# An encoder's attention: where the batch norm's fold-in is issued, and how the denominators of the first two blocks are summed

## Chip, cores, metric

One core of one Trainium2 chip. The metric is device time in microseconds from launch to end, as the median of several runs. Besides, one execution was profiled; its page and trace are what is read here. The engines are TensorE (PE, with its weight loads PEld), VectorE (DVE), ScalarE (ACT), GpSimd (POOL) and SyncE (SP); SP, ACT and POOL issue DMAs.

## What is computed

Two graph layers over 4096 nodes with 512 features in 4 heads of 128. The change lies in the first half of layer 0, the "encoder". Cut to what matters, with `adj` a 0/1 matrix of 4096 x 4096:

```python
Xw  = einsum('hnd,hde->hne', Xh, W)
f1, f2 = Xw . V[:, 0], Xw . V[:, 1]
sig = sigmoid(f1[:, :, None] + f2[:, None, :])
att = masked_softmax(adj * sig, adj != 0)        # local and long-range patterns are the same here
Xa  = einsum('hij,hjd->hid', att, Xw)            # per head
Xn  = batchnorm(Xa as (n, 512), gamma, beta)     # mean and variance over the nodes
emb = batchnorm(elu(Xn @ enc_W.T + enc_b) + Xn)
```

The decoder (`att` once more, on `emb`) and a GAT layer with its own attention follow; the change doesn't touch their instructions.

## The kernel before

The attention runs over 8 **blocks**: head h = 0 to 3, and for each head two halves of 2048 target nodes (`blocks`, n = 0 to 7; below block 1 to 8). Each block has 32 **tiles** j of 128 source nodes. A tile `e` is 128 sources x 2048 targets in fp32. It is made by tanh on ACT (line 419), exp on ACT (420) and a multiplication by the mask tile `a` on DVE (421). PE multiplies it with the values in four products of 512 targets (351; the fourth bank is only taken at tile EVICT = 2, which makes up for tiles 0 and 1 at 348).

Buffers for `e`: eight in turn, so that tile j + 8 is written where tile j was. Mask tiles: five buffers, loaded from DRAM by SP (199) out of a byte copy of the adjacency, which POOL's casting DMAs (450) write while the kernel starts. Every fifth tile (j = 4, 9, ...) is kept for the decoder by an `ekeep` DMA that ACT's queue issues at tile j + 3 (338).

The softmax's **denominators** are sums over the sources. There are three ways to add a tile, and the pair that `modes(n)` returns chooses: a tile in the first tuple ("moved") is added by an accumulating DMA of POOL into `acc2` (363); one in the second ("by ones") by four small ones-matmuls of PE into the bank `den` (303); any other by DVE into `acc` (371). At a block's end `acc` and `acc2`, if there is one, go through ones-matmuls too.

The **ending** of a block is spread over the next block's tiles by `at(j, ...)`: at tile 2 DVE evicts the four banks (520), at INVERT = 4 it copies `den`, and POOL writes it to DRAM and reads it back as a column (248, 250); at tile 10 `invert_them` inverts that on DVE (254, 255) and writes it (256); at tiles 11, 12, 18 and 19 `spread` loads it as rows `rb` (261), and six tiles after each DVE scales the output (524) and takes its statistics for the batch norm (527).

The batch norm is folded into the next product: `bn_coefs` (163) makes a and b from the statistics, with a square root on ACT (160) among DVE operations; b times the weights is added to the bias by 12 small matmuls (539, 541), and each row block of the weights `w` is multiplied by a (534). In block 8 the coefficients of heads 0 to 2 are ready to be made, and `three_heads` does all of that at one place, tile 16; the last head's follow in `last_head`.

All engines work through their instructions in a fixed order that the framework settles before the run, from the program's order, the data dependencies and the `pinned` hints.

Of the kernel before, what the change touches and what calls it, by code (L numbers as in the profile page):

```python
# [34 lines left out]
ALU = mybir.AluOpType  # L35
# [4 lines left out]
N, F, H, D, P = 4096, 512, 4, 128, 128  # L40
IB = 512
NIB = N // IB
NJ = N // P
C = IB // P

TB = 2048
NTB = N // TB
# [9 lines left out]
TINY = 1e-30  # L57
# [1 line left out]
G_MAX = 75.0  # L59


ENC_FIRST = (), (5, 6, 10, 11, 15, 16, 20, 21, 25, 26, 30, 31)
ENC = (0, 2, 5, 7, 10, 12, 15, 17, 20, 22, 25), (8, 9, 30, 31)
GAT = (0, 2, 5, 7, 10, 12, 15, 17, 20, 22, 25), (9, 30, 31)

# [4 lines left out]
EVICT = 2  # L70
INVERT = 4
# [9 lines left out]
def kernel(ctx, tc, x, xT, adjT, w0, w0T, v0, wencT, wdecT, vecs, w1, w1T, a1, outT):  # L81
    nc = tc.nc
# [11 lines left out]
    def nodes(r, ib):  # L94
        return r[:, ib * IB:(ib + 1) * IB]

    def block(r, j):
        return r[:, j * D:(j + 1) * D]

    def bank():  # L100
        return psum.tile([P, IB], FP, name="ps")

    def bank1():
        return psum1.tile([P, IB], FP, name="den")
# [10 lines left out]
    def vec_of(name):  # L115
        return vec[:, VECS.index(name), :]
# [21 lines left out]
    bias = consts.tile([P, C], FP, name="bias")  # L138
# [24 lines left out]
    def bn_coefs(st, gamma, beta, a, b, lo, hi):  # L163

        mv = consts.tile([P, C, 2], FP, name="bmv", bufs=2)
        for fb in range(lo, hi):
            nc.vector.bn_aggr(mv[:, fb, :], st[:, fb].rearrange("p c s -> p (c s)"))
        a, b, mv = a[:, lo:hi], b[:, lo:hi], mv[:, lo:hi]
        rsqrt(a, mv[:, :, 1], BN_EPS)
        nc.vector.tensor_mul(a, a, vec_of(gamma)[:, lo:hi])  # L170
        nc.vector.tensor_mul(b, mv[:, :, 0], a)
        return nc.vector.tensor_sub(b, vec_of(beta)[:, lo:hi], b)
# [37 lines left out]
    def attention(what, keep, pools, weights, values, row_of, out, finish, ebufs, modes=None, invert=None,  # L210
                  kept=None, sums=None, sums2=None, extras={}, row0=None, masks0=()):
# [20 lines left out]
        spool, made, masks0 = pools, 0, list(masks0)  # L232
# [11 lines left out]
        def denominators(h, tb, den):  # L244

            dsb = spool.tile([P, IB], FP, name="dsb")
            (nc.vector.tensor_copy if kept is not None else nc.scalar.copy)(dsb, den)
            nc.gpsimd.dma_start(dens[h][tb], dsb[0:P:32, :])
            dcol = spool.tile([P, TB // P], FP, name="dcol", bufs=2)
            nc.gpsimd.dma_start(dcol, dens[h][tb].rearrange("s (q k) -> (s q) k", k=TB // P))  # L250
            return dcol
# [6 lines left out]
        def spread(h, tb, s):  # L258

            rb = spool.tile([P, IB], FP, name="rb", bufs=2)  # L260
            nc.gpsimd.dma_start(rb, everywhere(rinvs[h][tb], 0, s * IB, IB))  # L261
            return rb

        def at(j, f, *args):

            later.setdefault(j, []).append(lambda: f(*args))

        def ending(h, tb, po, den):

            outs = [out(spool, h, tb, s, po[s]) for s in range(SB)]  # L270
            if den is not None:
                def invert_later():
                    dcol = denominators(h, tb, den)
                    at(INVERT + 6, invert_them, h, tb, dcol)

                at(INVERT, invert_later)
            rbs = {}
            for s, o in enumerate(outs):

                j = INVERT + 7 + s % 2 + s // 2 * 7  # L280
                at(j, lambda s=s: rbs.update({s: spread(h, tb, s)}))
                for k, f in enumerate(finish):
                    at(j + 6 + k, lambda f=f, s=s, o=o: f(spool, h, tb, s, o, rbs[s], False))
# [9 lines left out]
        for n, (h, tb) in enumerate(blocks):  # L293
            last = n == len(blocks) - 1
            moved, by_ones = modes(n) if modes is not None else ((), ())
            if invert is not None:
                den = bank1()
# [9 lines left out]
            po, ahead = [bank() for _ in range(SB - 1)], []  # L307
# [80 lines left out]
                else:  # L388
                    at(EVICT, nc.scalar.dma_start, ekeep[h][tb][k], t)
            if not last:  # L390
                at(EVICT, lambda *block_end: ending(*block_end), h, tb, po, den if invert is not None else None)
                rowb = next_row
                continue
            outs = [out(spool, h, tb, s, po[s]) for s in range(SB)]
# [31 lines left out]
    with tc.tile_pool(name="keep", bufs=1) as keep:  # L426

        with tc.tile_pool(name="f_small", bufs=1) as small, tc.tile_pool(name="f_work", bufs=2) as work:
# [5 lines left out]
            for ib in range(NIB):  # L434
# [7 lines left out]
                for c in range(0, C, 1 if ib == 0 else C):  # L442
                    n = 1 if ib == 0 else C
                    load = nc.sync.dma_start(xs[ib][:, c:c + n, :], xin[:, c:c + n, :])
# [10 lines left out]
            for ib in range(NIB):  # L455
# [39 lines left out]
                for c in range(C):  # L495
                    j = ib * C + c
# [7 lines left out]
                if ib == SB - 1:  # L504
                    store_rows(rows[0], targets(0))
                    row0 = keep.tile([P, TB], FP, name="rowb", bufs=2)
                    row0_load = load_row(row0, rows[0], 0)
                    with tc.issue_after(row0_load.ins):
                        masks0 = []
# [23 lines left out]
        def scale_weights(fb):  # L533
            nc.vector.tensor_scalar_mul(w[:, fb, :], w[:, fb, :], a_att[:, fb:fb + 1])  # L534

        def add_to_bias(pb, lo, hi, base):
            for o in range(C):
                for fb in range(lo, hi):
                    nc.tensor.matmul(pb[:, o:o + 1], w[:, fb, o * P:(o + 1) * P], b_att[:, fb:fb + 1],
                                     start=(fb == lo), stop=(fb == hi - 1))  # L540
            nc.vector.tensor_add(bias, pb[:, 0:C], base)

        def three_heads(load):
            bn_coefs(stats, "enc_bn_gamma", "enc_bn_beta", a_att, b_att, 0, C - 1)
            add_to_bias(bank(), 0, C - 1, vec_of("enc_mlp_b"))
            for fb in range(C - 1):
                scale_weights(fb)

        with tc.tile_pool(name="enc", bufs=1) as spool:

            with tc.issue_after(last_act.ins), tc.issue_after(masks0[-1][1].ins):
                attention("enc", keep, spool, tanh_weights, R[0:4], lambda h, tb: (rows[tb], h), out_enc,
                          (scaled, statistics), 6, lambda n: ENC if n > 1 else ENC_FIRST, (TINY, ALU.max), "write",
                          row0=row0, masks0=masks0,
                          extras={(2, 8): encoder_weights, (H * NTB - 1, NJ // 2): three_heads})


        def mlp_block(work, w, src, dst, gamma, beta, scale, between, early=None):
# [40 lines left out]
        with tc.tile_pool(name="m_small", bufs=1) as small, tc.tile_pool(name="m_work", bufs=3) as work:  # L599
            yc = [R[3]] + [small.tile([P, N], FP, name=f"yc{o}") for o in range(1, C)]  # L600

            def last_head():
                bn_coefs(stats, "enc_bn_gamma", "enc_bn_beta", a_att, b_att, C - 1, C)
                add_to_bias(bank1(), C - 1, C, bias)
                scale_weights(C - 1)

            mlp_block(work, w, xc, yc, "enc_mlp_bn_gamma", "enc_mlp_bn_beta", a_att, lambda o, ib: None, last_head)


            for h in range(H):  # L610
                w2 = work.tile([P, D], FP, name="w2", bufs=2)
                nc.vector.tensor_scalar_mul(w2, w0Ts[:, h, :], a_mlp[:, h:h + 1])
                bb = work.tile([P, P], FP, name="bb", bufs=1)
                nc.vector.tensor_scalar_mul(bb, ones, b_mlp[:, h:h + 1])
                pc = bank1()
                nc.tensor.matmul(pc[:, 0:D], bb, w0Ts[:, h, :], start=True, stop=True)
                cr = work.tile([P, 1, D], FP, name="cr", bufs=2)
                nc.vector.tensor_copy(cr[:, 0, :], pc[:, 0:D])
                for ib in range(NIB):
                    pv = bank().rearrange("p (c d) -> p c d", d=D)  # L620
                    for c in range(C):
                        nc.tensor.matmul(pv[:, c, :], block(yc[h], ib * C + c), w2, start=True, stop=True)  # L622
                    nc.vector.tensor_add(nodes(xc[h], ib).rearrange("p (c d) -> p c d", d=D), pv,
                                         cr.to_broadcast([P, C, D]))
# [17 lines left out]
        with tc.tile_pool(name="dec", bufs=1) as spool:  # L642
            attention("dec", keep, spool, tanh_weights, xc, lambda h, tb: (rows[tb], h), out_dec, (scaled, elu), 4,
                      kept="read")
# [5 lines left out]
    with tc.tile_pool(name="l_small", bufs=1) as small, tc.tile_pool(name="l_work", bufs=2) as work:  # L650
        x1 = [R[2]] + [small.tile([P, N], FP, name=f"x1_{o}") for o in range(1, C)]

        pb = bank1()
# [86 lines left out]
        for ib in range(NIB):  # L740
            for c in range(C):
# [3 lines left out]
                j = ib * C + c  # L745
# [18 lines left out]
            if ib == SB - 1:  # L764
                store_rows(rows1[0], targets(0))
                row0 = w.rearrange("p c f -> p (c f)")
# [61 lines left out]
    with tc.tile_pool(name="gat", bufs=1) as spool:  # L828
        x1_last = []

        def load_last(load):
            x1_last.append(spool.tile([P, TB], FP, name="rowb", bufs=2))
            nc.sync.dma_start(x1_last[0], outT[(H - 1) * P:H * P, (NTB - 1) * TB:NTB * TB])

        attention("gat", spool, spool, gat_weights, v1, lambda h, tb: (rowsg, tb * H + h), out_gat,
                  (scaled_gat, add_to_output), 7, lambda n: GAT, (N * TINY, ALU.add), sums=R[2][:, 0:TB],
                  sums2=row0, row0=row0,
                  extras={(0, 1): rest_of_rows, (H * NTB - 1, NJ - 10): load_last})
# [42 lines left out]
```

## Time and profile before

| | |
|---|---|
| runs | 3296.29 us median of 6 (3295.82 to 3298.07) |
| profiled execution | 3295.82 us, span 3293.7 us |
| granted TensorE clock | 0.992 |
| busy: PE, DVE, ACT, POOL | 3214.0, 2681.7, 2599.3, 331.8 us |
| tanh and exp on ACT | 1968 and 1879 ns each |
| multiplication by the mask, add to `acc`, DVE | 2260 and 2287 ns each |
| encoder's attention | from about 67 to 1063 us of the span |

A line of groups reads: line, engine, operation, output<-inputs, shapes, count, busy time, mean ns of one, idle time before and what ended it. A line of waits reads: who waited, for whom, total us, times, longest. A line of the timeline reads: start, length, engine, line, operation, and in brackets the wait before it and what ended it. The chain of waits follows the work that ended last back to what released it. Matmuls are pipelined, so busy PE is not PE at its peak.

### The profile page before, as it was taken

What the parts mean: (1) busy time and instruction counts of PE and PEld (TensorE: products, weight loads), DVE (VectorE), ACT (ScalarE), POOL (GpSimd) and SP (SyncE); (2) the same over time, 40 slices, a digit from 0 to 9 for tenths busy, and PEclk for the clock granted to TensorE, in tenths of its full rate; (3) what the DMA queues carried; (4) which work ended last, traced back from release to release, by engine and by line L of the source; (5) the groups of instructions that cost most, each with busy time, mean ns of one, the idle gap of its engine ahead of it and who ended that gap; (6) DMA issues with size and microseconds to landing.
All of it is one profiled execution on the core that took longest, in us unless ns stands there. A gap on an engine that the chain in (4) does not pass through costs nothing.

```text
span 3293.7 us, 25880 instructions
## 1 busy us (share of the span) xinstructions
PE 3214.0 (98%) x8847; PEld 1487.9 (45%) x8847; DVE 2681.7 (81%) x1919; ACT 2599.3 (79%) x1901; POOL 331.8 (10%) x478
## 2 busy tenths in 40 slices
PE   7999999999999999999999999999999999999999
PEld 6333444444443464444444444448644444444443
DVE  6889999999998665656655665585699999999997
ACT  7999999999997449999999999565756556666663
POOL 2000110110110000000000000025201111111111
PEclk9999999999999999999999999999999999999999
DMA  9994988988986013434443444231379779788976
GB/s 206 196 191 144 256 223 233 259 223 233 265 233 163 4 62 125 152 126 137 141 151 127 135 142 138 63 134 72 93 195 226 175 196 218 193 194 206 220 188 147
DMA packets 180164, 558.54 MB, mean 170 GB/s; under 512 B 20356, under 2 KB 23684, under 8 KB 144192
## 3 DMA queue, kind: packets, MB, share of 16 engines
q0 software_dynamic: 43088, 210.09, 33.3%
q1 hardware_dynamic: 126432, 293.72, 26.3%
q10 hardware_dynamic: 10512, 53.08, 3.9%
q8 instruction: 69, 1.13, 0.1%
q14 instruction: 63, 0.52, 0.0%
HBM read 378.15 MB, written 95.82 MB: 144 GB/s over the span
## 4 chain that ended last, share of the span: by engine, by line
PE 62%; DVE 16%; issue 8%; ACT 7%; DMA 6%; SPq 0%; DVEq 0%; POOL 0%; ACTq 0%; POOLq 0%
PE ps L351 49%; PE ps L566 7%; DVE e L421 6%; ACT e L419 4%; DMA a<-mask 3%; DVE e L808 3%; PE ps L750 3%; DVE R L371 3%; ACT e L420 2%; DVE acc L371 2%; PE den L303 1%; PE ps L622 1%; DMA R<-in_x 1%; PE ps L348 1%; DMA rb<-rinvs 1%
## 5 line engine op out<-in xcount | busy, mean ns | idle before, releaser
L351 PE MATMUL ps<-e,R 128*128 128x512 f32 x6048 | 2631.7, 596 | 44.4 <-DVE e L421 31.7
L351 PEld LDWEIGHTS ps<-e,R 128*128 128x128 f32 x6048 | 1146.7, 191 | 1521.7 <-issue 1420.0
L421 DVE TENSOR_TENSOR e<-e,a 128x2048 f32<-128x2048 f32 (+1 forms) x470 | 1052.1, 2260 | 385.3 <-ACT e L420 363.3
L419 ACT ACTIVATE e<-rowb,score 128x2048 f32<-128x2048 f32 (+1 forms) x470 | 912.9, 1968 | 98.3 <-PE ps L351 58.1
L420 ACT ACTIVATE e<-e 128x2048 f32<-128x2048 f32 (+1 forms) x470 | 871.0, 1879 | 15.9 <-DVE e L421 9.7
L807 ACT ACTIVATE e<-rowb,nq,jcol 128x2048 f32<-128x2048 f32 x224 | 458.2, 2087 | 230.5 <-DMA w<-e 142.9
L808 DVE SCALAR_TENSOR_TENSOR e<-e,jcol,a 128x2048 f32<-128x2048 f32 (+1 forms) x259 | 592.5, 2326 | 2.6 <-ACT e L807 2.6
L371 DVE TENSOR_TENSOR R<-R,e 128x2048 f32<-128x2048 f32 x128 | 293.3, 2292 | 0.0
L371 DVE TENSOR_TENSOR acc<-acc,e 128x2048 f32<-128x2048 f32 x126 | 288.2, 2287 | 2.1
L566 PE MATMUL ps<-R,w 128*128 128x512 f32 x512 | 220.3, 592 | 0.6 <-DVE w L534 0.6
L261 POOL DMA_DIRECT2D rb<-rinvs x88 | 59.1, 687 | 1104.6 <-DVE R L524 894.6
L566 PEld LDWEIGHTS ps<-R,w 128*128 128x128 f32 x512 | 97.2, 190 | 122.7 <-issue 118.2
L363 POOL DMA_DIRECT2D w<-e x77 | 64.7, 841 | 645.8 <-DMA w<-e 268.5
L750 PE MATMUL ps<-w1x,hT 128*128 128x260 f32 x512 | 118.0, 390 | 1.8 <-ACT hT L723 1.8
L586 ACT ACTIVATE ex<-ps,bias 128x512 f32<-128x512 f32 x64 | 44.0, 688 | 95.4 <-PE ps L566 78.3
L363 POOL DMA_DIRECT2D acc<-e x66 | 55.8, 845 | 572.0 <-DMA acc<-e 167.0
L750 PEld LDWEIGHTS ps<-w1x,hT 128*128 128x128 f32 x512 | 98.3, 193 | 21.5 <-ACT hT L723 3.4
L807 ACT ACTIVATE e<-w,nq,jcol 128x2048 f32<-128x2048 f32 (+1 forms) x35 | 65.3, 1936 | 31.9 <-DMA dacc<-e 31.9
L820 ACT ACTIVATE R<-R,vec 128x512 f32<-128x512 f32 x32 | 23.0, 720 | 70.3 <-DVE R L817 70.2
L588 DVE SCALAR_TENSOR_TENSOR ex<-ex,re 128x512 f32<-128x512 f32 x64 | 45.0, 703 | 35.8 <-ACT re L587 35.6
L303 PE MATMUL den<-e,ones 128*32 128x512 f32 x584 | 70.9, 599 | 0.0
L755 ACT ACTIVATE R<-ps,rstd 128x128 f32<-128x128 f32 x128 | 38.5, 369 | 39.5 <-PE ps L750 37.3
(163 smaller groups left out, 1267.4 us busy)
## 6 DMA issues: line engine op xcount, KB each, us to landing
a<-mask SPq DMA_DIRECT2D x720, 256.0 KB, 3.6
w<-e POOLq DMA_DIRECT2D x77, 1024.0 KB, 8.3
acc<-e POOLq DMA_DIRECT2D x66, 1024.0 KB, 8.7
ekeep<-e ACTq DMA_DIRECT2D x48, 1024.0 KB, 5.5
e<-ekeep SPq DMA_DIRECT2D x48, 1024.0 KB, 4.8
rb<-rinvs POOLq DMA_DIRECT2D x88, 256.0 KB, 5.4
mask<-in_adjT POOLq DMA_DIRECT2D x8, 2048.0 KB, 103.7
rowb<-rows SPq DMA_DIRECT2D x16, 1024.0 KB, 4.9
```

The lines of the kernel that those rows point to most:

```text
L261: nc.gpsimd.dma_start(rb, everywhere(rinvs[h][tb], 0, s * IB, IB))
L303: last_ones = nc.tensor.matmul(den[s * 32:(s + 1) * 32, :], ones[:, 0:32], t[:, s * IB:(s + 1) * IB], start=not begun, stop=stop)
L351: last_main = nc.tensor.matmul(b, block(values[h], j), e[:, s * IB:(s + 1) * IB], start=(j == 0), stop=(j == NJ - 1))
L363: nc.gpsimd.dma_start(sums2 if n else dacc, e, **({"accum_op": ALU.add} if j > moved[0] else {}))
L371: nc.vector.tensor_add(acc, acc, e)
L419: nc.scalar.activation(e, rowb, AF.Tanh, bias=column(score[:, 1], j, h), scale=0.5)
L420: last_act = nc.scalar.activation(e, e, AF.Exp, scale=0.5)
L421: last_dve = nc.vector.tensor_mul(e, e, a)
L566: nc.tensor.matmul(z, w[:, fb, o * P:(o + 1) * P], nodes(src[fb], ib), start=(fb == 0), stop=(fb == C - 1))
L750: nc.tensor.matmul(b[:, 0:2 * DX], hT[:, fb, c * P:(c + 1) * P], w1x[:, fb, 2 * k:2 * k + 2, :].rearrange("p h x -> p (h x)"), start=(fb = ...
L807: last_act = nc.scalar.activation(e, rowb, AF.Relu, bias=column(nq, j, h), scale=column(jcol, j, h))
L808: last_dve = nc.vector.scalar_tensor_tensor(e, e, column(jcol2, j, h), a, ALU.add, ALU.mult)
```

## The change

It has four parts.

1. Block 1: the ones-tiles become 6, 7, 14, 15, 22, 23, 30 and 31 (eight in place of twelve). The other 24 tiles are added by DVE.
2. Block 1's ending, which runs in block 2: `slack` = 4, so `invert_them`, `spread` and what follows them come four tiles later. The endings of the other blocks stay.
3. Block 2: six tiles are moved by DMA (13, 15, 17, 20, 22, 25), six stay with PE (5, 6, 10, 11, 30, 31).
4. Block 8: `three_heads` becomes `coefs_of_three` at tile 10, `bias_of_three` at tile 12 and `scale_three` (bias addition and scaling of the weights) at tile 20. The bias matmuls' bank is held from 12 to 20.

```diff
-ENC_FIRST = (), (5, 6, 10, 11, 15, 16, 20, 21, 25, 26, 30, 31)
+ENC_FIRST = (), (6, 7, 14, 15, 22, 23, 30, 31)
+ENC_SECOND = (13, 15, 17, 20, 22, 25), (5, 6, 10, 11, 30, 31)
 ENC = (0, 2, 5, 7, 10, 12, 15, 17, 20, 22, 25), (8, 9, 30, 31)
...
-        def ending(h, tb, po, den):
+        def ending(h, tb, po, den, slack):
...
-                    at(INVERT + 6, invert_them, h, tb, dcol)
+                    at(INVERT + slack + 6, invert_them, h, tb, dcol)
...
-                j = INVERT + 7 + s % 2 + s // 2 * 7
+                j = INVERT + slack + 7 + s % 2 + s // 2 * 7
...
-                at(EVICT, lambda *block_end: ending(*block_end), h, tb, po, den if invert is not None else None)
+                at(EVICT, ending, h, tb, po, den if invert is not None else None,
+                   4 if kept == "write" and n == 0 else 0)
...
-        def add_to_bias(pb, lo, hi, base):
+        def bias_of(pb, lo, hi):
             for o in range(C):
                 for fb in range(lo, hi):
                     nc.tensor.matmul(pb[:, o:o + 1], w[:, fb, o * P:(o + 1) * P], b_att[:, fb:fb + 1],
                                      start=(fb == lo), stop=(fb == hi - 1))
-            nc.vector.tensor_add(bias, pb[:, 0:C], base)
-
-        def three_heads(load):
+            return pb
+        banks = []
+        def coefs_of_three(load):
             bn_coefs(stats, "enc_bn_gamma", "enc_bn_beta", a_att, b_att, 0, C - 1)
-            add_to_bias(bank(), 0, C - 1, vec_of("enc_mlp_b"))
+        def bias_of_three(load):
+            banks.append(bias_of(bank(), 0, C - 1))
+        def scale_three(load):
+            nc.vector.tensor_add(bias, banks[0][:, 0:C], vec_of("enc_mlp_b"))
             for fb in range(C - 1):
                 scale_weights(fb)
...
-                          (scaled, statistics), 6, lambda n: ENC if n > 1 else ENC_FIRST, (TINY, ALU.max), "write",
-                          row0=row0, masks0=masks0,
-                          extras={(2, 8): encoder_weights, (H * NTB - 1, NJ // 2): three_heads})
+                          (scaled, statistics), 6, lambda n: (ENC_FIRST, ENC_SECOND, ENC)[min(n, 2)],
+                          (TINY, ALU.max), "write", row0=row0, masks0=masks0,
+                          extras={(2, 8): encoder_weights, (H * NTB - 1, 10): coefs_of_three,
+                                  (H * NTB - 1, 12): bias_of_three, (H * NTB - 1, 20): scale_three})
```

The last head's `last_head` adds its bias in the same way as before, spelled with `bias_of`.

More of the change, by code (lines that the diff above doesn't have):

```diff
@@ L603, in last_head @@
                 bn_coefs(stats, "enc_bn_gamma", "enc_bn_beta", a_att, b_att, C - 1, C)
-                add_to_bias(bank1(), C - 1, C, bias)
+                nc.vector.tensor_add(bias, bias_of(bank1(), C - 1, C)[:, 0:C], bias)
                 scale_weights(C - 1)
```

## The prediction

> Blocks are numbered 1 to 8 as in the title (n = 0 to 7 in the code), tiles 0 to 31 in a block. The forecast is a small gain, 3286.6 us against 3296.29 us.
>
> **What bounds the kernel now.** I cut the encoder's attention at the start of each block's first tanh on ACT and asked for busy time by stretch. The columns are length, then busy time (count) of PE, weight loads, DVE, ACT and POOL, then TensorE clock, DMA share and GB/s. The rows are blocks 1, 2, 4, 7 and 8 (the last short of its final exp).
>
> ```profile
> 67.20:189.00 121.80, 111.12 (x311) 45.10 (x311) 104.28 (x58) 121.60 (x83) 0.00 (x0) 0.97 1.05 188
> 189.00:320.00 131.00, 126.63 (x360) 51.63 (x359) 123.61 (x68) 118.82 (x65) 3.89 (x7) 0.97 0.66 163
> 440.50:559.20 118.70, 116.18 (x305) 49.66 (x304) 114.57 (x65) 118.58 (x65) 13.24 (x18) 1.00 0.88 237
> 796.80:915.90 119.10, 116.55 (x306) 49.85 (x305) 114.94 (x65) 118.82 (x65) 13.20 (x18) 1.00 0.87 239
> 915.90:1040.80 124.90, 118.59 (x321) 51.24 (x320) 112.71 (x74) 119.59 (x67) 13.18 (x18) 0.97 0.84 225
> ```
>
> A steady block is ACT-bound: ACT is busy 118.58 of 118.70 us (tanh 1.97 plus exp 1.88 us per tile), with PE and DVE 2 to 4 us below. Blocks 2 and 8 stick out, by 12 and 6 us, while ACT has no more work there. What ACT waits for comes from the waits of two stretches: the first line is of 67 to 189 us, the others of 189 to 330 us; the numbers are total, times, longest.
>
> ```profile
> DVE e L421 <- DMA a<-mask: 8.3, 2, 6.6
> ...
> ACT e L420 <- DVE e L421: 6.3, 2, 3.8
> ACT e L419 <- DVE e L421: 4.9, 1, 4.9
> DVE dcol L254 <- DMA dcol<-dens: 4.4, 1, 4.4
> DVE e L421 <- DMA a<-mask: 2.7, 2, 1.7
> ```
>
> ACT loses 11.2 us to DVE in block 2. These are stores of kept tiles: ACT issues the `ekeep` DMA of tile j when it is three tiles on, in order with its activations, and that DMA waits for DVE's multiplication of j. Once DVE is over 11 us behind ACT, ACT stops. DVE itself lost 11.0 us to mask loads (8.3 + 2.7) and 4.4 us to the read-back of the first denominators. The chain of waits (start, length) shows both:
>
> ```profile
> 139.75 22.82 DMA a<-mask
> ...
> 165.01 17.41 DMA a<-mask
> ...
> 189.47 16.01 DMA a<-mask
> ...
> 239.78 6.44 DMA dcol<-dens
> ```
>
> While the adjacency is copied (DMA share 1.05 in block 1) a mask takes 16 to 23 us, and with five mask buffers the load for tile j+5 is issued when tile j is multiplied. That loop, not DVE's work, sets the pace from 140 to 206 us. In block 8 the timeline (start, length, engine, what; in brackets the wait) shows the batch norm of three heads:
>
> ```profile
> 983.98 0.20 ACT L160 ACTIVATE coefs<-coefs 128x3 f32<-128x3 f32 x1 [1.87 <-DVE coefs L159]
> ...
> 992.66 2.73 PE L539 MATMUL ps<-coefs,w 128*128 128x1 f32 x24
> ...
> 994.99 0.49 DVE L534 TENSOR_SCALAR w<-w,coefs 128x512 f32<-128x512 f32 x1 [7.58 <-PE ps L539]
> ...
> 1007.41 1.91 ACT L420 ACTIVATE e<-e 128x2048 f32<-128x2048 f32 x1 [3.34 <-DVE e L421]
> ```
>
> PE is some two tiles behind, the bias matmuls stand behind its backlog, and DVE, whose scaling of `w` must wait for them, stands 7.58 us; the ACT stall of 3.34 us is again a store behind a late multiplication. Ahead of that DVE has room, waiting twice for ACT (tiles 10 and 13):
>
> ```profile
> 958.54 4.50 DVE L421 TENSOR_TENSOR e<-e,a 128x2048 f32<-128x2048 f32 x2 [2.04 <-ACT e L420]
> ...
> 969.76 4.50 DVE L421 TENSOR_TENSOR e<-e,a 128x2048 f32<-128x2048 f32 x2 [2.20 <-ACT e L420]
> ```
>
> **The Trainium skill.** "VectorE: DVE Perf Modes", section "The TRN2 errata", prices an fp32 add of 2048 elements at 2291 ns; the accumulator adds here take 2287 ns. "ScalarE: Activation LUTs", section "What ACT_TABLE_LOAD costs", gives 1283 ns for the load plus about 1380 ns of drain per switch; here a load takes 1283 ns and starts 0.01 us after the tanh before it, so I price a switch at 1.28 us. "DMA: Bandwidth & Descriptors", section "Issuing engines are not separate DMA queues", says that transfers of SP, ACT and POOL interleave on the same engines; the mask loads above agree, since they land 2.5 us after issue at best, 11.3 in the median of 67 to 320 us. "TensorE: Matmul & The Clock Gate", Part 3, says that column tiles run concurrently; the 16 instructions of two ones-tiles take 1.92 us together, so a ones-tile costs PE about 0.95 us, not four full matmuls.
>
> **Part 1, fewer ones-tiles in block 1.** Tiles 5, 10, 11, 16, 20, 21, 25, 26 become DVE adds; 7, 14, 22, 23 become ones-tiles. PE loses 4 x 0.95 = 3.8 us, which I cost at nothing: DVE and the masks release PE there. DVE gains 4 x 2.29 = 9.2 us. Pushing the adds through the list of starts, DVE has four extra by tile 21 and is ready for tile 22 at 164.0 instead of 156.1 us (two short waits of 0.5 and 0.7 us swallow the rest); before, it waited there until 162.7. Tiles 22 and 23 then give two adds back, 25 and 26 take them again, within the 1.75 us mask wait at tile 27 and the 0.99 and 1.74 us at the next block's first two tiles. So the cover is the 11.0 us of mask waits. What can leak is the loop: tile 17's multiplication, which releases tile 22's load, ends 1.8 us later by the same count. If loads are limited by bandwidth, nothing moves; if by latency, all later landings move 1.8 us. I take 0.9. If the cover were gone altogether, block 2 would start 8 us later on DVE.
>
> **Part 2, first denominators later.** In block 2 `invert_them` moves from tile 10 to 14, the four `spread` loads and their eight DVE operations four tiles on. The read-back landed at 246.2 us, since the 8 KB write queued behind the last adjacency copies; DVE gets to tile 14 near 254 us. The 4.4 us wait goes, and nothing takes its place: invert, `rinvs`, `rb` (1 to 10 us each on POOL) have seven tiles, 27 us, until the first scaling at tile 21, and the last statistics come at tile 30.
>
> **Part 3, six moved tiles in block 2.** DVE keeps 19 adds. PE drops six ones-tiles and gains one for the DMA's sum: 5 x 0.95 = 4.8 us less, in a stretch (251 to 390 us) where the chain runs through a saturated PE. Of this I count 1.1 us: DVE's four waits for the evicted banks at 334 us. POOL gains six 1 MB accumulating DMAs, after the copies have ended at 239 us; each takes some 8.7 us to land and holds its buffer until then. A buffer is wanted again eight tiles (31 us) later. In block 4 the same six run beside six more with no ACT wait, so I cost them at nothing (they only add, so below nothing is excluded; the upper end is rival (c)). Queued behind a moved tile on POOL are `rinvs` and `rb`; their seven tiles cover it. The next block's first moved tile now waits for PE's last denominator, as in blocks 4 to 8 already (up to 25 us on POOL, ACT not held).
>
> Blocks 1 to 3: DVE, the bound until ACT leads again in block 3, gains 4.4 + 1.1 - 0.9 = **4.6 us**. ACT could gain 6.3 in block 2 and 1.5 in block 3 (waits for PE's denominator, 1.0, and an accumulating DMA, 0.5), so DVE's figure decides. The 4.9 us stall at block 2's tile 8 stays: it comes from tile 4, ahead of every edit but Part 1.
>
> **Part 4, block 8.** Coefficients at tile 10, bias matmuls at 12, scaling at 20. PE's 24 matmuls (2.73 us) find coefficients some 10 us old; DVE's scaling comes some 25 us after them; the bank is held eight tiles longer with four of seven others in use. From tile 13 DVE works without a pause, so its chain sets the end: block 8's last multiplication ends 138.1 us after the block's first tanh (915.9 to 1054.0), block 4's 127.7 us (440.5 to 568.2). The 10.4 us between are the wait of 7.58, the aggregate and small operations (0.82 and 0.79) and 1.6 of bias and scaling. The 1.6 stays; the aggregate falls into the 2.04 and 2.20 us of room. But the square root costs ACT two table loads and 0.20, 2.77 us, plus a wait of 0 to 1.87. At tile 17 DVE was late anyway; at tile 10 it follows ACT at once, so 2.8 to 4.6 us enter the chain, 3.7 taken. 10.4 - 1.6 - 3.7 = **5.1 us**, between 4.2 and 6.0.
>
> **The sum.** 4.6 + 5.1 = 9.7 us. The profiled execution took 3295.82 us (span 3293.7, 2.1 around it), 0.5 below the median; so it would be 3286.1, the median 3286.6.
>
> **The rivals.** (a) The mask loop doesn't absorb the adds: 8 us late on DVE by block 2. DVE then reaches the read-back after 246.2 us, so the 4.4 us wait would have gone anyway; blocks 1 to 3 lose 8 - 4.4 - 1.1 = 2.5, block 8 gains 5.1, in all 3293.7. For it: the chain alternates mask and multiplication. Against: a DMA share of 1.05 says that bytes, not requests, set landings. (b) The end is ACT's: all 7.8 us of blocks 2 and 3 and 6 of block 8 come back, 3282.5. For it: PE gets lighter. Against: nothing shortens DVE's list. (c) Slower: POOL's queue. If a `spread` that waits for DVE's first scaling (19.8 us now) is put ahead of the moved tiles 17 to 22, their buffers come back late: a tile is ready some 16 us after its tanh began, 8.7 to land leaves 6 us, and the rest of 19.8 is 13.8 us of ACT wait; a second one at tile 23 adds up to 5. Against 9.7 of gain that is 4 to 9 us more than now: about 3303. It decides once such a hold exceeds 6 us. Against: in block 4 moved tiles are issued ahead of the same loads. (d) A part has no effect, because the static order puts the new steps where the old stood: block 8 or block 2 alone gains, about 3291.5.
>
> **The numbers.** 0.2% is 6.6 us, about what a measurement of this kernel can tell from no change: faster means below 3289.7. Forecast 0.60, (a) 0.12, (b) 0.14, (c) 0.07, (d) 0.07. The forecast's own bounds (3.7 to 5.5 and 4.2 to 6.0) all lie beyond the line; for an order of instructions that I can't foresee I leave an eighth of it short of it. Faster 0.60 x 7/8 + 0.14 = 0.66, slower 0.07 from (c), same 0.27. The range 3281.0 to 3295.0 holds all but (c) and the edges.
>
> **What would show it.** Right: block 2 near 125 us with no `dcol` wait and ACT's later two stalls gone; mask waits in blocks 1 and 2 shrunk to 2 or 3 us with block 1's ACT time unchanged; block 8 near 121 us with no DVE wait at L534. Wrong: ACT waits in block 1, ACT waiting for an accumulating DMA in block 2, or block 8's ACT waiting for the square root by more than 2 us.

## The result, and the profile after

The changed kernel takes 3285.62 us in the median (20 runs, 3278.94 to 3292.59), the kernel before 3295.85 us beside it (40 runs). The ratio is 0.9971, with a 95% interval of 0.9965 to 0.9977: 9.6 us less, between 7.6 and 11.5. The forecast was 9.7 us less. Its parts did not come out as forecast, though, as the profile after already shows.

Its span is 3284.2 us. Not all of the 9.5 us to the span before is the change's: the first tanh starts at 63.6 instead of 67.2 us, ahead of every edit, and 3.2 us lie behind the last multiplication of block 8. Between the two this profile is only 2.7 us shorter (984.1 against 986.8): 6.2 less in block 8, but 1.4 more in blocks 1 to 3, and 2.1 more in blocks 4 to 7, which no edit touches. One profile of each kernel thus doesn't place the gain; what each part is worth is taken from the timed runs of the experiments, and the profiles say which waits came and went.

In the changed kernel the same steps stand on other lines: tanh, exp and the multiplication on 422, 423 and 424, the products on 352, the ones-matmuls on 304, the moved tiles on 364, DVE's adds on 372. These are the stretches of blocks 1, 2, 3, 4 and 8 (length; busy time and count of PE, weight loads, DVE, ACT, POOL; clock, DMA share, GB/s):

```profile
63.60:185.40 121.80, 108.73 (x283) 44.88 (x283) 112.06 (x62) 121.60 (x82) 0.00 (x0) 0.97 1.05 189
185.40:312.80 127.40, 121.99 (x322) 51.09 (x320) 125.37 (x68) 119.07 (x65) 8.97 (x13) 1.00 0.93 219
312.80:438.30 125.50, 119.29 (x306) 50.32 (x307) 116.15 (x65) 118.99 (x66) 13.20 (x18) 0.99 0.87 238
438.30:557.00 118.70, 114.80 (x301) 48.70 (x300) 112.70 (x63) 118.57 (x65) 13.18 (x18) 1.00 0.88 237
915.80:1035.70 119.90, 118.10 (x324) 51.87 (x322) 114.28 (x75) 119.72 (x68) 13.20 (x18) 0.99 0.86 235
```

Block 3 of the kernel before was this:

```profile
320.00:440.50 120.50, 119.89 (x308) 51.57 (x307) 115.14 (x65) 118.89 (x66) 13.23 (x18) 1.00 0.88 245
```

Block 8 went from 124.9 to 119.9 us and block 2 from 131.0 to 127.4, but block 3 from 120.5 to 125.5: the first three blocks together take 374.7 us against 373.3. The waits of block 1 (first line), of block 2 (next three) and of block 3 (last two) say where:

```profile
DVE e L424 <- DMA a<-mask: 1.6, 2, 1.2
...
ACT e L422 <- DVE e L424: 3.9, 1, 3.9
ACT e L422 <- DMA acc<-e: 2.6, 2, 2.3
...
DVE e L424 <- DMA a<-mask: 1.7, 1, 1.7
...
POOL acc L364 <- DMA acc<-e: 41.8, 5, 12.4
...
ACT e L422 <- DMA acc<-e: 6.4, 3, 3.3
```

The wait for the read-back (`dcol`) and ACT's two later stalls behind stores are gone, mask waits fell from 11.0 to 3.4 us (1.6 + 1.7, rounded), and block 1 still takes 121.80 us. ACT now waits for buffers which accumulating DMAs hold, 2.6 us in block 2 and 6.4 in block 3 (before, 0.5 in block 3 alone). The timeline of block 3 from 379 us on, ACT, POOL and SP alone (start, length, what, wait before):

```profile
379.17 2.00 ACT L422 ACTIVATE e<-rowb,score 128x2048 f32<-128x2048 f32 x1 [3.33 <-DMA acc<-e]
...
379.61 0.88 POOL L364 DMA_DIRECT2D acc<-e  x1 [10.25 <-DMA acc<-e]
...
380.56 1.22 SPq L193 DMA_DIRECT2D rowb<-rows  x1
...
392.40 2.00 ACT L422 ACTIVATE e<-rowb,score 128x2048 f32<-128x2048 f32 x1 [1.90 <-DMA acc<-e]
...
392.87 0.85 POOL L364 DMA_DIRECT2D acc<-e  x1 [12.38 <-DMA acc<-e]
```

Each accumulation waits for the one before. ACT's first wait, 3.33 us, ends as the accumulation issued at 368.42 lands, ahead of the row load. The next one, issued at 379.61, runs beside that 1 MB load (380.56) and takes 12.7 us, against 8.6 in the median; ACT's wait of 1.90 us at 392.40 ends as it lands. In block 8 the three steps stand apart:

```profile
957.92 0.20 ACT L161 ACTIVATE coefs<-coefs 128x3 f32<-128x3 f32 x1
...
961.38 4.50 DVE L424 TENSOR_TENSOR e<-e,a 128x2048 f32<-128x2048 f32 x2 [2.46 <-ACT e L423]
...
969.66 2.84 PE L542 MATMUL ps<-coefs,w 128*128 128x1 f32 x24
...
972.60 4.50 DVE L424 TENSOR_TENSOR e<-e,a 128x2048 f32<-128x2048 f32 x2 [2.20 <-ACT e L423]
...
1001.66 1.27 DVE L537 TENSOR_SCALAR w<-w,coefs 128x512 f32<-128x512 f32 x3
```

The square root waits for nothing, the scaling at 1001.66 carries no wait (7.58 before), and DVE still has its two gaps. From the block's first tanh to its last multiplication it takes 131.9 us (915.8 to 1047.7), against 138.1.

### The profile page after: what moved, and what is told of

Read it like the earlier page. It is cut to its first block, busy times and chain, and to the rows that moved or that the text cites. A ratio compares the mean times of both kernels' runs of the same rounds, so it can differ in the third digit from the quotient of the medians.

```text
span 3284.2 us, 25758 instructions
## 1 busy us (share of the span) xinstructions
PE 3203.1 (98%) x8775; PEld 1485.7 (45%) x8775; DVE 2691.9 (82%) x1923; ACT 2598.8 (79%) x1901; POOL 336.1 (10%) x484
## 4 chain that ended last, share of the span: by engine, by line
PE 67%; DVE 14%; ACT 7%; issue 7%; DMA 5%; SPq 0%; DVEq 0%; ACTq 0%; POOL 0%; POOLq 0%
PE ps L352 52%; DVE e L424 7%; PE ps L579 7%; ACT e L422 4%; PE ps L763 3%; DVE acc L372 3%; ACT e L423 2%; DMA a<-mask 2%; PE den L304 1%; DMA acc<-e 1%; DVE e L821 1%; DVE R L372 1%; PE ps L349 1%; PE ps L635 1%; DMA R<-in_x 1%
## 5 line engine op out<-in xcount | busy, mean ns | idle before, releaser
L372 DVE TENSOR_TENSOR acc<-acc,e 128x2048 f32<-128x2048 f32 x130 | 297.3, 2287 | 2.1
L304 PE MATMUL den<-e,ones 128*32 128x512 f32 x504 | 61.3, 599 | 0.0
```

What stands on the lines that cost most here:

```text
L304: last_ones = nc.tensor.matmul(den[s * 32:(s + 1) * 32, :], ones[:, 0:32], t[:, s * IB:(s + 1) * IB], start=not begun, stop=stop)
L372: nc.vector.tensor_add(acc, acc, e)
```

## Experiments

Two theories stood at the start. **Parts**: blocks 1 to 3 and block 8 gain about half each. **Block 8 alone**: the profile after shows no gain in blocks 1 to 3. All gains below are against the kernel before on the same chip, from the ratio times 3296 us, with the interval.

**Part 4 alone.** `ENC_FIRST`, `ENC_SECOND` and the slack set back:

```diff
-ENC_FIRST = (), (6, 7, 14, 15, 22, 23, 30, 31)
-ENC_SECOND = (13, 15, 17, 20, 22, 25), (5, 6, 10, 11, 30, 31)
+ENC_FIRST = ENC_SECOND = (), (5, 6, 10, 11, 15, 16, 20, 21, 25, 26, 30, 31)
-                   4 if kept == "write" and n == 0 else 0)
+                   0)
```

> The kernel before with Part 4 alone (block 8's batch norm at tiles 10, 12 and 20). The prediction's theory: 5.1 us less, 4.2 to 6.0; block 8's DVE wait at the weights' scaling (7.6 us) gone, ACT waiting 0 to 1.9 us for the square root. Rival (the profile of the changed kernel shows blocks 1 to 3 no shorter than before): the whole gain of some 10 us is this part's, and it shows 8 to 11 us less.

Ratio 0.9982 (0.9974 to 0.9990): 5.9 us less (3.3 to 8.6). The "Parts" theory holds for it; it is not the whole gain.

**Parts 1 to 3 alone.** Block 8's steps joined again at tile 16:

```diff
-extras={..., (H * NTB - 1, 10): coefs_of_three, (H * NTB - 1, 12): bias_of_three, (H * NTB - 1, 20): scale_three}
+extras={..., (H * NTB - 1, NJ // 2): three_heads}     # the three steps one after the other
```

> The kernel before with Parts 1 to 3, block 8 as before. The prediction's theory: 4.6 us less (3.7 to 5.5), no wait for the denominators' read-back, mask waits of 2 to 3 us. Rival: the six accumulating DMAs hold buffers until ACT waits for them, as in the profile after (2.6 us in block 2, 6.4 in block 3), and the part brings nothing: 0 to 2 us less.

Ratio 0.9990 (0.9982 to 0.9998): 3.3 us less (0.7 to 5.9). It lies between the two expectations, and its profile has ACT waiting 11.3 us for accumulating DMAs from 60 to 440 us. That profile, of the slowest of its 13 runs, takes 377.1 us for blocks 1 to 3, longer than the 373.3 before; like the profile of the whole change, it doesn't show where the timed runs gain. So the parts were taken apart further.

**Part 2 alone**, and **Parts 1 and 2**, both with block 8 as before and no moved tiles in block 2:

```diff
 # Part 2 alone: both sets as in the kernel before, slack 4 kept
 # Parts 1 and 2: ENC_FIRST as changed, and
-ENC_SECOND = (13, 15, 17, 20, 22, 25), (5, 6, 10, 11, 30, 31)
+ENC_SECOND = (), (5, 6, 10, 11, 15, 16, 20, 21, 25, 26, 30, 31)
```

> The kernel before with Part 2 alone (first denominators inverted four tiles later). The prediction's theory: the 4.4 us wait of DVE goes and nothing is late next, 4.4 us less; ACT's two later stalls in block 2 (6.3 us) shrink. Rival: DVE's freed time is used up by a PE that is saturated from 251 us on, 0 to 1 us less.

> The kernel before with Parts 1 and 2, no moved tiles in block 2. The prediction's theory: 4.4 less 0.9 of leak, 3.5 us less. If the moved tiles cost more than they bring, this is the fastest of the set e2 to e4, 5 us less or more; if the masks don't absorb the four adds, it is 2 us slower than Part 2 alone or worse.

Part 2 alone: 0.9980 (0.9971 to 0.9989), 6.6 us less (3.6 to 9.6). Parts 1 and 2: 0.9977 (0.9968 to 0.9985), 7.6 us less (4.9 to 10.5), 4.3 more than with the moved tiles on top (3288.27 against 3292.07 us in the median, on one chip). So the moved tiles cost. The waits of ACT behind stores in block 2 with Part 2 alone keep only the early stall:

```profile
ACT e L422 <- DVE e L424: 4.9, 1, 4.9
```

In that profile block 2 takes 124.7 us instead of 131.0, but block 3 123.4 instead of 120.5; ACT waits there 3.1 us for PE's reading of the denominators (1.0 before) and 1.2 for an accumulating DMA.

**Without Part 3.** The whole change, block 2's set as in the last diff:

> Parts 1, 2 and 4, without the moved tiles of block 2 (its twelve ones-tiles as before). If the parts add up as measured alone (Parts 1 and 2 -7.6, Part 4 -5.9), 13 us less than before, some 3 us faster than the whole change; ACT waits for no accumulating DMA in block 3. The prediction's own theory, in which Part 3 brings 1.1 us, expects it 1 us slower than the whole change, at about 9 us less.

0.9958 (0.9945 to 0.9970): 13.8 us less (9.9 to 18.1), 4.3 faster than the whole change, as in the pair before. The parts add up (7.6 + 5.9 = 13.5).

**Why the moved tiles cost.** Two candidates: block 3's first moved tile now waits for PE to read the shared sum (theory S), or the load of the encoder's weights, which falls on block 3's first accumulations (theory W).

```diff
 # S (shortened): a sum of its own for block 2, in a half of R[4]; PE reads it from there
-nc.gpsimd.dma_start(sums2 if n else dacc, e, ...)
+nc.gpsimd.dma_start(R[4][:, TB:2 * TB] if n == 1 else sums2 if n else dacc, e, ...)
 # W
-extras={(2, 8): encoder_weights, ...
+extras={(1, 11): encoder_weights, ...
```

> The whole change, but block 2's moved tiles are summed in a tile of their own (the half of R[4] that is free then), so that block 3's first moved tile need not wait for PE to read block 2's sum. Theory S: this wait (22 us on POOL) starts block 3's chain of eleven accumulating DMAs some 5 us late, and that is what makes ACT wait there; then block 3's ACT waits on accumulating DMAs (6 to 8 us) fall to 2 or less and the kernel is 3 to 5 us faster than the whole change, 13 to 15 us less than before. Theory W: the load of the encoder's weights in the same block does it; then only 0 to 2 us change.

> The whole change, with the 1 MB load of the encoder's weights issued at tile 11 of block 2 in place of tile 8 of block 3. Theory W: that load beside the first moved tiles of block 3 lengthens its chain of accumulating DMAs, so block 3's ACT waits shrink from 6 to 8 us to 2 or less and 3 to 5 us are won against the whole change. Theory S (late start because of the shared sum): block 3 keeps at least 4 us of these waits.

Own sum: 0.9979 (0.9971 to 0.9988), 6.9 us less: no gain on the whole change. Block 3's first accumulation does start some 5 us earlier (11.5 us after the block's tanh instead of 16.2), but the next one comes 21.8 us after that tanh, as in the whole change, right beside the weights' load, and ACT waits longer. Its lines of block 3, waits first, then timeline:

```profile
ACT e L427 <- DMA acc<-e: 10.8, 4, 3.9
```

```profile
329.15 2.48 DVE L528 COPY R<-ps 128x512 f32<-128x512 f32 x4 [3.45 <-PE den L309]
...
334.12 0.86 POOL L369 DMA_DIRECT2D acc<-e  x1 [9.77 <-DVE e L429]
334.23 0.43 SPq L538 DMA_DIRECT2D w<-in_wencT  x1
```

The first of these shows that this run is no clean test of theory S. The half of R[4] is not free long enough: DVE evicts block 2's output into it at block 3's tile 2 and must now wait 3.45 us until PE has read the sum, which the whole change doesn't have; with that DVE, and the multiplication that the second accumulation adds, come later.

Early weights: 0.9957 (0.9945 to 0.9969), 14.2 us less (10.2 to 18.1). In its block 3 ACT's wait is nearly gone:

```profile
ACT e L422 <- DMA acc<-e: 1.1, 2, 0.9
```

Block 3's first accumulation starts some 16 us after the block's first tanh here too, so theory S, which expected 4 us of waits to stay, fell by this run. Theory W's expectation was met: block 3 takes 120.2 us instead of 125.5, while block 2, where the load now falls, takes 129.7 instead of 127.4 (4.8 us of such ACT waits).

But the load is not the cause by itself. In the kernel before and in the one without Part 3 it also comes 0.1 us after block 3's second accumulation, which then takes 13.1 and 12.9 us to land (11.9 in the whole change). ACT waits 0.5 us for accumulating DMAs in that block of the kernel before, and without Part 3 no more than this:

```profile
ACT e L422 <- DMA acc<-e: 1.7, 2, 1.0
```

So in these runs the load shows a cost only together with Part 3. The profiles show one thing that goes with the waits: in the four kernels where ACT waits over 6 us there (the whole change, Parts 1 to 3, own sum, and the later steps of block 8 below), the accumulation of block 3's tile 12 is issued within 1 us of the row load, in all others 3 us or more ahead of it. That is a coincidence of times in single profiles. No run moved the row load, or took Part 3's lighter PE apart from its six transfers, so how Part 3 and the load make the cost together stays open.

**Without Part 3, early weights.** Both edits together:

> Parts 1, 2 and 4 without moved tiles in block 2, and the encoder's weights loaded at tile 11 of block 2. If that load costs block 3 only where moved tiles precede it, the same as Parts 1, 2 and 4 (13.9 us less than before, within 2). If it also lengthens block 3's chain without them (1.7 us of ACT waits are left there), 15 to 16 us less.

0.9953 (0.9941 to 0.9965): 15.5 us less. Beside 13.8 without the early weights and 14.2 with Part 3 this is inside the intervals. So with the weights early Part 3 makes no difference that the timed runs can tell; in the single profiles blocks 1 to 3 still take longer with it, 371.7 against 367.3 us.

**More adds in block 1**, to see what covers them. On the kernel without Part 3:

```diff
-ENC_FIRST = (), (6, 7, 14, 15, 22, 23, 30, 31)
+ENC_FIRST = (), (30, 31)
```

> Parts 1, 2 and 4 without moved tiles, and six more of block 1's ones-tiles turned into DVE adds (only 30 and 31 stay). If the mask waits are the cover that the prediction names, 3.4 us of it are left, so 6 x 2.29 = 13.7 us of adds make DVE 10 us later at block 2: mask waits of 1 us or less in blocks 1 and 2, ACT stalls by late stores in block 1 and 2 up by 8 to 10 us, 4 us less than the kernel before (8 to 12 us slower than Parts 1, 2 and 4). If DVE's adds in block 1 are hidden by something else (a slower PE, the copies), it stays within 3 us of Parts 1, 2 and 4.

0.9989 (0.9983 to 0.9996): 3.6 us less, so 10.2 us of gain lost. Block 1 takes 130.7 us instead of 121.8. Mask waits are gone from its blocks 1 and 2, and ACT's stalls behind stores are back (waits from 66 to 321 us):

```profile
ACT e L423 <- DVE e L424: 8.9, 3, 3.6
...
ACT e L422 <- DVE e L424: 3.2, 1, 3.2
```

The mask waits are the cover, and they are used up.

**Block 8, unsplit at tile 10.** On the kernel before, `three_heads` at tile 10:

> The kernel before with block 8's three steps together at tile 10 in place of tile 16. If the gain of Part 4 is the distance between the steps, DVE waits at the scaling for PE's backlog again, 12 to 14 us at tile 10, where PE is 9 us behind; 2.2 us of that fit into DVE's room, and block 8 takes 137 to 140 us from its first tanh to its last multiplication: the same as before within 2 us, 5 to 6 us slower than Part 4 alone. If the earlier place is what gains, it is as fast as Part 4 alone (131.9 us, 5.9 us less than before).

0.9997 (0.9989 to 1.0005): no change. Its DVE timeline in block 8 shows why:

```profile
972.78 0.16 DVE L557 TENSOR_TENSOR bias<-ps,vec 128x4 f32<-128x4 f32 x1 [7.98 <-PE ps L542]
```

The wait was 8 us, not the 12 to 14 expected, since one multiplication went ahead of it; block 8 took 137.7 us to its last multiplication. So the distance between the steps gains, not the earlier place. Which of the two distances is needed, from the coefficients to the bias or from there to the scaling, wasn't tried.

**Block 8, later.** The whole change with the steps moved, and the same on the kernel without Part 3 with early weights:

```diff
-(H * NTB - 1, 10): coefs_of_three, (H * NTB - 1, 12): bias_of_three, (H * NTB - 1, 20): scale_three
+(H * NTB - 1, 17): coefs_of_three, (H * NTB - 1, 19): bias_of_three, (H * NTB - 1, 26): scale_three
```

> The whole change, with block 8's coefficients at tile 17, bias at 19, scaling at 26. Where ACT is ahead of DVE, the two table loads and the square root (2.77 us) leave the chain, and the coefficients' DVE work (1.6 us) enters it: block 8 from its first tanh to its last multiplication 131 us in place of 131.9, 1 us less than the whole change, not to be told apart by the clock. If ACT's loss there is not hidden, 133 us or more.

> As Parts 1, 2 and 4 without moved tiles and with the early weights, and block 8's steps at tiles 17, 19 and 26. Either place of the steps gave the same block 8 (131.9 and 132.1 us), so it is within 2 us of the same kernel with tiles 10, 12 and 20: 13 to 16 us less than before. If the late place frees the end of block 8 (its last product ended 138.9 in place of 140.6 us after the first tanh), 1 to 2 us faster.

On the whole change: 0.9964 (0.9952 to 0.9977), not to be told from it; block 8 took 132.1 us to its last multiplication, not 131. The 1 us expected did not show. But its last product ended 138.9 us after the first tanh instead of 140.6, and so it did in the second kernel. That one has the lowest median of all: 3278.68 us, ratio 0.9949 (0.9936 to 0.9961), 16.8 us less than before and 7 below the change, though its interval overlaps that of the same kernel with tiles 10, 12 and 20 (15.5). The end of its block 8 and that of the same kernel with tiles 10, 12 and 20, DVE and PE alone:

```profile
1033.22 2.28 DVE L424 TENSOR_TENSOR e<-e,a 128x2048 f32<-128x2048 f32 x1
1035.42 2.28 DVE L372 TENSOR_TENSOR acc<-acc,e 128x2048 f32<-128x2048 f32 x1
1037.62 4.69 DVE L424 TENSOR_TENSOR e<-e,a 128x2048 f32<-128x2048 f32 x5
1039.45 1.92 PE L304 MATMUL den<-e,ones 128*32 128x512 f32 x16
```

```profile
1030.27 4.61 DVE L372 TENSOR_TENSOR acc<-acc,e 128x2048 f32<-128x2048 f32 x2
1034.79 6.89 DVE L424 TENSOR_TENSOR e<-e,a 128x2048 f32<-128x2048 f32 x6
1037.13 3.70 PE L352 MATMUL ps<-e,R 128*128 128x512 f32 x8 [1.80 <-DVE e L424]
1040.76 1.92 PE L304 MATMUL den<-e,ones 128*32 128x512 f32 x16
```

In the first, the order on DVE came out otherwise: tile 30 is multiplied before the last add, so PE is done with its products when the last tile comes. In the second, 3.7 us of products of tile 30 stand ahead of the ones-matmuls. I didn't separate this order from the place of the steps.

## Why the prediction was right, and where it was not

The total was right (9.7 against 9.6 us), in part by luck, since errors offset each other: Part 3 was to bring 1.1 us and cost 4.3, while Parts 1 and 2 together brought 7.6 (4.9 to 10.5) where the sum has 4.4 - 0.9 = 3.5, and Part 4 5.9 where it has 5.1.

- **Part 1, the cover: held.** Mask waits shrank from 11.0 to 3.4 us and block 1 kept its length. Measured from the block's first tanh, block 2's second multiplication starts at 138.3 us, as before (138.4), so the leak for which I took 0.9 doesn't show. Six more adds, beyond that cover, lost 10.2 us, against 10 worked out from the waits left. Parts 1 and 2 together measured 1 us better than Part 2 alone, which these runs can't tell from none. Rival (a) is out.
- **Part 2: right cause, probably sized too small.** 4.4 us forecast, 6.6 measured (3.6 to 9.6); that interval holds 4.4, but the one of Parts 1 and 2 together doesn't hold the 3.5 forecast for them. The step in doubt is "DVE's figure decides": in the profiles ACT's two later stalls, 6.3 us, went altogether and not only by DVE's 4.4, and block 2 became 6.3 us shorter, of which block 3 gave 2.9 back.
- **Part 3: the failing step is "so I cost them at nothing".** I had compared with block 4, where eleven moved tiles run without ACT waits, and took that as showing room. It cost 4.3 us, in both pairs of kernels that differ by it. It was not rival (c), a `spread` holding up POOL: no such wait is in block 2 of the profile after. ACT waited for the transfers, mostly in block 3. That block, unlike block 4, has the 1 MB load of the weights beside its first accumulations, and without that load there the waits went; but the load costs nothing like it where Part 3 is absent, so the mechanism is only half known. The forecast's list of wrong signs named ACT waits on accumulating DMAs in block 2; the larger share came in block 3.
- **Part 4: held.** 5.1 forecast, 5.9 alone. The square root waited 0 of the "0 to 1.87", so its loss on ACT was 2.8 and not 3.7. In the profile block 8 gave 6.2 us by the same count, just above the upper bound of 6.0. (The pieces that the forecast names for its 10.4 us, 7.58, 0.82, 0.79 and 1.6, add up to 10.8.) That this loss matters at tile 10 and not at 17 was not borne out: the late place gave no shorter chain of multiplications.
- Rival (b), in which ACT's waits come back whole, describes the kernels without Part 3 better than the change: the two with block 8's steps at tiles 10, 12 and 20 took 3280.6 and 3283.2 us where it had 3282.5.
- Blocks 1 to 3 together: 4.6 forecast, 3.3 measured, inside the interval but as 7.6 less 4.3. The single profile after shows less than that (374.7 against 373.3 us), and is one execution of a kernel whose runs spread over 14 us.

## What to carry to other kernels

When a dependent chain crosses three engines (DVE, ACT, PE, DVE), issue its steps so far apart that none of them waits behind the next engine's backlog; moving the whole batch earlier gained nothing here. An engine's waits are a budget for work handed to it: count what is left of them. Here 9.2 us of adds fitted into 11.0 us of waits, and 13.7 us more, with 3.4 left, cost 10.2. Before calling a chain of serialized DMAs free because another stage carries it, list the other large transfers of the stage it is to run in.

## What the runs showed of the hardware

A 1 MB accumulating DMA took 8.6 us in the median from issue to landing in the changed kernel. Where a 1 MB load of SP's queue was issued within 1 us of it, which happens 17 times in the profiles of all these kernels, it took 12.7 to 14.8 us; where the row load followed 3 to 6 us later, mostly about 10 (8.5 to 12.2). The load can be slowed too: the rows at 380.56 took 12.1 us, against 8.4 in the median of the encoder's eight. Each accumulation into one tile waited for the one before, as the timeline of block 3 shows, so such a meeting can put off those behind it. A switch of ACT's table there and back around a square root cost 2.77 us in all, with no drain to be seen between the neighbouring activations.
